# Spreading the output projections over single cycles, and moving the low-bit check of the weights, in an attention and feed-forward kernel

## The chip, the cores and the metric

The kernel runs on one core of a Trainium2 chip. The metric is the device time of one launch in microseconds (us), the median over several runs. Below, PE is TensorE (matrix products), DVE is VectorE, ACT is ScalarE, POOL is GpSimd and SP is SyncE, whose queue issues nearly all DMAs of this kernel.

## The reference, cut to what matters

```python
# x: (2, 1024, 512); 32 query heads, 8 key/value heads, head size 16
Q, K, V = x @ Wq.T + bq, x @ Wk.T + bk, x @ Wv.T + bv      # then split in heads
Q, K = _rope(Q, K);  K, V = repeat(K, 4), repeat(V, 4)
w = softmax(Q K^T / sqrt(16))
x = _layernorm(x + (w V) @ Wo.T + bo)                      # attention, post-norm
g = (x @ gate_w.T) * gate_s                                # gate_w, up_w: (1408, 512), ternary
u = (x @ up_w.T) * up_s
x = _layernorm(x + ((silu(g) * u) @ down_w.T) * down_s)    # down_w: (512, 1408), ternary
```

Everything is float32.

## The kernel before

**Attention.** The work is cut into 32 units: 2 batches, 2 halves of 512 queries, 8 key/value heads. A unit has 8 steps of 128 keys, so there are 256 steps, and the main loop takes two steps in each of its 128 cycles (`for c in range(STEPS // 2)`). For numerical reasons each score is made twice. The A pass (`max_pass`, L390) makes the scores with the queries in rows, and DVE reduces each to its maximum (`mx<-pa`, L398), 8 reductions a cycle; it runs 12 steps ahead (`LEAD`). The B pass (`exp_pass`, L432) makes the scores with the keys in rows, and ACT takes the exponential (L440). Then `av` (L453) multiplies by the values. After each unit `max_rows` (L405 to L414) brings the maxima into row form, by way of memory. In the last 6 cycles the A passes are all done (`alone`).

**Fills.** Into the head of each cycle (the letter F of the written order `WITH_FILL`) one piece of other matrix work is put, taken from the list `fill`. Up to cycle 28 these are the projections and transposes of Q, K and V. From cycle 36 on they belong to the rest of the layer, a quarter of 512 rows at a time. Quarter q starts at cycle 32(q + 1) + 4. It consists of the output projections (`project`, L560: four row tiles `t` of 128 rows), the transposition of the normalised rows (`x1_turn`, L592), 22 gate and up products (`hidden`, L611, in 11 blocks `f`, gate and then up), and four down products (`down`, L686, one for each row tile, 22 matmuls each). A quarter has 32 cycles, and this list has 30 entries, as each `project` handles two row tiles. So in two cycles of each of the first two quarters there is no fill, and the order is `NO_FILL`. Four quarters exist; the last one (`LASTQ`) has no attention left to lie beside, and is done after the loop, in a tail. The tail also takes the last two down products of quarter 2: the loop stops taking fills when two are left.

**The written order.** The order of instructions on every engine is that of the program (`tc.manual_schedule`); each engine executes its own in that order, and waits where an operand isn't ready. Small work (normalisation, gating, stores) is put off with `after(n, f)`, and is emitted at one of two points of each cycle, V0 and V1, by `v_hook`. V1 is about two thirds into the attention part of a cycle. SP's DMAs stand in one queue in that same order, so a DMA that waits for its data holds back those after it.

**Banks and buffers.** Seven PSUM banks go round among fills, A and B passes (`take` and `leave`); an eighth collects `av`. Weight tiles `wt` for the gate and up products are read from memory, one for each product, into a ring of `RING = 5` buffers; `hidden(i)` asks for tile i + RING - 1. The rows to which the attention's output is added are loaded by `load_residual` (DMA and an addition on POOL), of which the pool `fp5` holds five; the next quarter's are asked for by `more`, after the down products' rows are stored.

**Low bits.** The feed-forward weights are also rounded to a reduced format (float32r) in the first quarter of the loop: 33 pieces of 128x512 are loaded (`piece_load`, L174 and L179), rounded on ACT (`piece_round`, L184) and stored (L191). To see whether the rounding lost anything, DVE ORs the low 12 bits of each piece into a tile `low` (L186). `low_flag` reduces that tile to one number, in cycle 29. If it is not zero, the kernel does the whole feed-forward part again at full precision at the end (`feed_forward`); with the ternary weights of the reference it is zero.

Of the kernel before, what the change touches and what calls it, by code (L numbers as in the profile page):

```python
# [7 lines left out]
F32 = mybir.dt.float32  # L8
I32 = mybir.dt.int32
F32R = mybir.dt.float32r  # L10
AF = mybir.ActivationFunctionType
ALU = mybir.AluOpType
# [4 lines left out]
P = 128  # L17
B, T, D = 2, 1024, 512
# [6 lines left out]
NF = INTER // P  # L25
# [5 lines left out]
TH = HALF // P  # L31
# [6 lines left out]
US = NT  # L38
STEPS = len(UNITS) * US
QS = HKV * US  # L40
RING = 5
PIECES = 3 * NF
LOW = 0xFFF
LEAD = 12
# [2 lines left out]
def attn_ffn_kernel(tc, x, wqkv, bqkv, wo, bo, rope, wg, wu, wd, gs, us, ds, out):  # L47
    nc = tc.nc

    def pool(name, bufs=1, **kw):  # L50
        return tc.alloc_tile_pool(name=name, bufs=bufs, **kw)
# [7 lines left out]
    ap3 = pool("ap3", 3)  # L59
    wp = pool("wp", RING, side="right")  # L60
    qp1 = pool("qp1", side="right")
# [19 lines left out]
    def bank(name, shape=(P, HALF)):  # L81
        if psf[0] is None:
            return take("F", name, shape)
        p, tag = psf[0]
        return p.tile(list(shape), F32, tag=tag, name=name)
# [77 lines left out]
    low = ap1.tile([P, D], I32, name="low")  # L163
    flag = base.tile([1, 1], I32, name="flag")
    nc.gpsimd.memset(low, 0)
    SW, SR = {}, {}

    def piece_load(i):
        if i >= PIECES:
            return  # L170
        SW[i] = sp4.tile([P, D], F32, tag="sw", name="sw")
        if i < 2 * NF:
            f, up = divmod(i, 2)
            nc.sync.dma_start(  # L174
                out=SW[i].rearrange("p (c n) -> p c n", n=P),
                in_=(wu if up else wg)[:, :, f * P : (f + 1) * P],
            )
        else:
            nc.sync.dma_start(out=SW[i], in_=wd[:, i - 2 * NF, :])  # L179

    def piece_round(i):
        w = SW.pop(i)
        SR[i] = sp4.tile([P, D], F32R, tag="sr", name="sr")
        nc.scalar.copy(SR[i], w)  # L184

        nc.vector.scalar_tensor_tensor(  # L186
            low, w.bitcast(I32), LOW, low, ALU.bitwise_and, ALU.bitwise_or
        )

    def piece_store(i):  # L190
        nc.sync.dma_start(out=wsd[i], in_=SR.pop(i).bitcast(F32))  # L191
# [13 lines left out]
    def after(n, f):  # L205
        later.setdefault(now[0] + n, []).append(f)
# [237 lines left out]
    LASTQ = B * NH - 1  # L444
# [107 lines left out]
        mv, rs = sums(row)  # L552
        e.tensor_scalar(row, row, mv[:, 0:1], rs, ALU.subtract, ALU.mult)

    def project(q, t0):
        two = (t0, t0 + 1)
        py = {t: bank("py") for t in two}
        for c in range(NC):
            for t in two:
                nc.tensor.matmul(  # L560
                    py[t],
                    NUM[q, c][:, t * P : (t + 1) * P],
                    wo_sb[:, c, :],
                    start=c == 0,
                    stop=c == NC - 1,
                )
        for t in two:
            add_rows(q, t, py[t])
# [36 lines left out]
    def hidden(q, f, up):  # L605
# [3 lines left out]
        for c in range(NC):  # L609
            for k, x1 in enumerate(FP["x1"]):  # L610
# [6 lines left out]
                )  # L617
        ask_weights(i + RING - 1)
        if not up:
# [60 lines left out]
    def down(q, t, f0=0, f1=NF):  # L680
        if f0 == 0:
            FP["d", t] = bank("pd")
        pd = FP["d", t]
        for f in range(f0, f1):
            for k, h in enumerate(FP["h"]):
                nc.tensor.matmul(  # L686
                    pd,
                    h[:, f, t * P : (t + 1) * P],
                    wd_sb[:, f, :],
                    start=f == 0 and k == 0,  # L690
                    stop=f == NF - 1 and k == 1,
                )
        if f1 < NF:
            return
        end = q == LASTQ or now[0] >= 2 * STEPS
        ys = (FP["tmp"] if end else fp1).tile([P, D], F32, tag="ys", name="ys")
        if end:
            nc.vector.tensor_tensor(ys, pd, dsb, ALU.mult)
            nc.vector.tensor_tensor(XQ[q, t], ys, XQ[q, t], ALU.add)
            mv, rs = sums(XQ[q, t])  # L700
        else:
            nc.scalar.copy(ys, pd)
            nc.gpsimd.tensor_tensor(ys, ys, dsb, ALU.mult)
            nc.gpsimd.tensor_tensor(XQ[q, t], ys, XQ[q, t], ALU.add)
            after(2, lambda: norm(XQ[q, t], nc.gpsimd))

        def store():
            if end:
                row = XQ[q, t]
                nc.vector.tensor_scalar(row, row, mv[:, 0:1], rs, ALU.subtract, ALU.mult)  # L710
            b, qh = divmod(q, NH)
            r = qh * TH + t
            nc.sync.dma_start(out=out[b, r * P : (r + 1) * P, :], in_=XQ.pop((q, t)))
            after(2, more)

        def more():

            for i in range(TH):
                if q < LASTQ and (q + 1, i) not in DONE and i <= t + 1:
                    DONE.add((q + 1, i))  # L720
                    load_residual(q + 1, i)

        after(2 if end else 5, store)


    fill = [lambda m=m: qk_block(0, 1, m) for m in range(1, QK // P - 1)]
# [15 lines left out]
    fill = [(0, f) for f in fill]  # L742

    def quarter(q):
        first = (q + 1) * QS // 2 + 4
        fs = [lambda t=t: project(q, t) for t in (0, 2)]
        fs += [lambda t=t: (x1_turn(q, t), x1_turn(q, t + 1)) for t in (0, 2)]
        for f in range(NF):
            for up in (0, 1):
                fs.append(lambda a=(q, f, up): hidden(*a))  # L750
        downs = [(t, 0, NF) for t in range(TH)]
        if q == LASTQ:

            downs = [(0, 0, NF - 1), (1, 0, NF - 1), (0, NF - 1, NF), (1, NF - 1, NF), (2, 0, NF)]
        for a in downs:
            fs.append(lambda a=a: down(q, *a))
        if q == LASTQ:
            fs.append(lambda: last_down(q, TH - 1))
        return [(first, f) for f in fs]
# [89 lines left out]
    for c in range(STEPS // 2):  # L849
        probs = {}  # L850

        pieces = range(*(min(max(0, (i - 2) * PIECES // (QS // 2 - 5)), PIECES) for i in (c, c + 1)))
        for i in pieces:
            piece_round(i)
        if pieces:
            after(1, lambda ps=pieces: [(piece_store(i), piece_load(i + 4)) for i in ps])
        alone = 2 * c + LEAD >= STEPS
        has_fill = bool(fill) and fill[0][0] <= c
        if c >= (STEPS - QS) // 2:
            has_fill = has_fill and len(fill) > 2  # L860
        for s in NO_A if alone else WITH_FILL if has_fill else NO_FILL:
            if s == "F":
                if has_fill:
                    fill.pop(0)[1]()
                    leave("F")
                continue
            n = 2 * c + int(s[-1])
            if s[0] == "V":
                v_hook(n)
                if before is not None:  # L870
                    av(n - 2, before[n - 2])
                continue
            j, i = int(s[1]), "abc".index(s[2])
            if s[0] == "A":
                max_pass(n + LEAD, j, i)
                continue
            if i == 2 and n not in probs:
                probs[n] = ap3.tile([P, G, HALF], F32, tag="prob", name="prob")
            exp_pass(n, j, i, probs.get(n))
        before = probs  # L880
        u, s = divmod(2 * c + 1, US)
        if s == US - 1 and u + 3 < len(UNITS):
            prep(u + 3)
        if (2 * c + 1 + LEAD) % US == US - 1 and not alone:
            max_rows((2 * c + 1 + LEAD) // US)
        if 0 <= (f := c - QS // 2 - 4) < NF:
            nc.sync.dma_start(out=wd_sb[:, f, :].bitcast(F32), in_=wsd[2 * NF + f])
        if c == QS // 4:
            load_weights()
        if c == QS // 2 - 3:  # L890
            low_flag()
        if c == QS // 2 - 2:
            sp4.release()
            qp4.release()
            qp2.release()
            qp1.release()
            fp1 = pool("fp1", side="right")
            fp4 = pool("fp4", 4, side="right")
            fp5 = pool("fp5", 5, side="right")
            wd_sb = fp1.tile([P, NF, D], F32R, name="wd_sb")  # L900
            FP["tmp"] = fp1
            for i in range(RING):
                after(i + 11, lambda i=i: ask_weights(i))
            for t in range(TH):
                after(t + 1, lambda t=t: load_residual(0, t))
            for q in range(B * NH - 1):
                fill.extend(quarter(q))
# [11 lines left out]
    ps_x = pool("ps_x", 8, space=PSUM)  # L919
    psf[0] = (ps_x, "px")  # L920

    del fill[-2:]
    rest = [(0, lambda a=a: down(LASTQ - 1, *a)) for a in ((2, 0, NF), (3, 0, 8), (3, 8, NF))]
    last = quarter(LASTQ)
    while later:
        v_hook(min(later))
    fill += [rest[0], *last[0:2], rest[1], *last[2:4], rest[2]]
    n = 2 * STEPS

    def drain():  # L930
# [135 lines left out]
```

## Time and profile before

| | |
|---|---|
| Median of 3 runs | 1137.92 us (1136.79 to 1137.92) |
| The profiled execution: its own time | 1135.88 us |
| its span, first to last instruction | 1134.0 us |
| mean granted clock of TensorE | 0.997 |
| busy: PE, DVE, ACT, POOL | 1109.4, 819.3, 703.4, 384.1 us |
| first quarter of the loop and cycles 29 to 35 | to 322.92 us |
| quarter 0, quarter 1 (from the first projection to the next quarter's) | 252.21, 252.20 us |
| DVE's low-bit operations (33, from 82.4 to 272.8 us) | 23.7 us |

The times of the stages are read from the chain of waits in order of time, in which each fill of a cycle has a row with its start. A fill's row starts a cycle, so the distance of two such rows is the length of a cycle. The busy time of PE is modelled at the ends of instructions, so the lengths of cycles tell more than the busy share.

### The profile page before, as it was taken

The page shows a single profiled execution, that of the slowest core. Times are in us where ns is not written, and L with a number is a line of the kernel's source. Part 1 is how long each engine was busy: PE and PEld are TensorE (multiplying, and loading weights), DVE is VectorE, ACT ScalarE, POOL GpSimd, SP SyncE. Part 2 cuts the span into 40 slices and gives each one's busy share as a digit, 9 for nine tenths or more (in the row PEclk, how much of TensorE's full clock was granted, in tenths as well). Part 3 has the DMA queues.
Part 4 walks back from the last instruction along what each step waited for, and adds up shares of the span by engine and source line. Part 5 has one row for each costly group of instructions (what it writes and reads, how often), then busy time and mean ns, then how long its engine had stood idle before and what let it go on. Part 6 is the DMA issues. An engine that isn't in the chain of part 4 may idle for free.

```text
span 1134.0 us, 23242 instructions
## 1 busy us (share of the span) xinstructions
PE 1109.4 (98%) x8894; PEld 590.9 (52%) x8894; DVE 819.3 (72%) x1481; ACT 703.4 (62%) x1312; POOL 384.1 (34%) x411
## 2 busy tenths in 40 slices
PE   7999999999999999999999999999999999999997
PEld 5534545555444555555544555555544555545686
DVE  4968888988867777776658777776668778722634
ACT  3148777776746777775547777775537777783251
POOL 4473441442124222223524222224535222235332
PEclk9999999999999999999999999999999999999999
DMA  6577666664424332220222222220323222111331
GB/s 180 165 240 229 198 216 204 211 212 147 87 68 146 123 115 85 83 84 30 81 86 97 86 86 86 83 87 24 98 66 106 87 87 87 50 53 66 105 118 40
DMA packets 98919, 127.60 MB, mean 113 GB/s; under 512 B 26873, under 2 KB 51194, under 8 KB 98674
## 3 DMA queue, kind: packets, MB, share of 16 engines
q1 hardware_dynamic: 98450, 125.72, 36.1%
q8 instruction: 72, 1.18, 0.4%
q10 hardware_dynamic: 352, 0.33, 0.1%
q14 instruction: 45, 0.37, 0.1%
HBM read 83.56 MB, written 36.93 MB: 106 GB/s over the span
## 4 chain that ended last, share of the span: by engine, by line
PE 89%; DVE 8%; issue 1%; POOL 0%; ACT 0%; DMA 0%; ACTq 0%; POOLq 0%; SPq 0%; DVEq 0%
PE pv L453 21%; PE pa L390 21%; PE pg L611 15%; PE pb L432 13%; PE pd L686 7%; DVE mx L398 5%; PE py L560 5%; PE pq L259 5%; DVE st L539 1%; PE pv L318 1%; PE pt L244 1%; PE px L592 0%; PE pd L661 0%; DVE xq L582 0%; DVE rot L280 0%
## 5 line engine op out<-in xcount | busy, mean ns | idle before, releaser
L398 DVE TENSOR_REDUCE mx<-pa 128x1 f32<-128x512 f32 x1024 | 646.3, 684 | 174.9 <-PE pa L390 104.1
L440 ACT ACTIVATE prob<-pb 128x512 f32<-128x512 f32 x1024 | 540.7, 600 | 198.8 <-PE pb L432 157.4
L390 PE MATMUL pa<-KS,QH 32*128 32x512 f32 x1024 | 334.7, 449 | 4.1 <-DVE mx L398 2.9
L432 PE MATMUL pb<-QH,KS 32*128 32x512 f32 x1024 | 304.1, 460 | 4.9 <-DVE mx L398 4.2
L390 PE MATMUL pa<-KS,QL 32*128 32x512 f32 x1024 | 306.9, 407 | 0.0
L453 PE MATMUL pv<-prob,va 128*32 128x512 f32 x2048 | 272.9, 604 | 0.0
L432 PE MATMUL pb<-QL,KS 32*128 32x512 f32 x1024 | 271.3, 417 | 0.0
L432 PE MATMUL pb<-mt,ones 32*128 32x512 f32 x1024 | 243.4, 394 | 0.0
L390 PEld LDWEIGHTS pa<-KS,QH 32*128 32x128 f32 x1024 | 145.7, 182 | 156.5 <-DVE mx L398 109.1
L642 POOL TENSOR_TENSOR z<-pus,z 128x512 f32<-128x512 f32 x44 | 56.4, 1283 | 389.4 <-ACT pus L639 362.3
L432 PEld LDWEIGHTS pb<-QL,KS 32*128 32x128 f32 x1024 | 127.3, 183 | 93.4 <-issue 92.2
L390 PEld LDWEIGHTS pa<-KS,QL 32*128 32x128 f32 x1024 | 158.6, 183 | 19.0 <-issue 9.2
L432 PEld LDWEIGHTS pb<-QH,KS 32*128 32x128 f32 x1024 | 129.6, 182 | 31.4 <-DVE mx L398 18.6
L611 PE MATMUL pg<-x1h,wt 128*128 128x512 f32 x352 | 144.6, 411 | 0.0
L432 PEld LDWEIGHTS pb<-mt,ones 32*128 32x128 f32 x1024 | 138.8, 183 | 2.0
L611 PE MATMUL pg<-x1l,wt 128*128 128x512 f32 x352 | 137.9, 392 | 0.3 <-DVE x1l L596 0.3
L453 PEld LDWEIGHTS pv<-prob,va 128*32 128x32 f32 x2048 | 40.8, 108 | 93.5 <-issue 82.0
L611 PEld LDWEIGHTS pg<-x1h,wt 128*128 128x128 f32 x352 | 66.0, 187 | 37.1 <-issue 11.6
L259 PE MATMUL pq<-xT,wqkv_sb 128*128 128x256 f32 (+1 forms) x248 | 79.5, 462 | 3.4 <-DVE xT L247 1.2
L611 PEld LDWEIGHTS pg<-x1l,wt 128*128 128x128 f32 x352 | 66.2, 188 | 12.8 <-DVE x1l L596 0.8
L277 POOL TENSOR_TENSOR t<-q,cosT 128x256 f32<-128x256 f32 (+1 forms) x31 | 31.0, 999 | 108.9 <-ACT q L275 106.3
L686 PE MATMUL pd<-wd_sb,hh 128*128 128x512 f32 x165 | 66.0, 400 | 0.7 <-ACT o L469 0.7
(100 smaller groups left out, 1013.5 us busy)
## 6 DMA issues: line engine op xcount, KB each, us to landing
wt<-wsd SPq DMA_DIRECT2D x88, 256.0 KB
KS<-kT SPq DMA_DIRECT2D x124, 128.0 KB
wsd<-sr SPq DMA_DIRECT2D x33, 256.0 KB
QH<-qT SPq DMA_DIRECT2D x31, 256.0 KB
QL<-qT SPq DMA_DIRECT2D x31, 256.0 KB
qT<-hi SPq DMA_DIRECT2D x18, 256.0 KB
qT<-lo SPq DMA_DIRECT2D x18, 256.0 KB
xs<-in_x_dram SPq DMA_DIRECT2D x16, 256.0 KB
```

The lines of the kernel that those rows point to most:

```text
L244: nc.tensor.transpose(pt[:, c, :], xs[:, c * P : (c + 1) * P], ident)
L259: nc.tensor.matmul(pq, wqkv_sb[:, c, m * P : (m + 1) * P], XT[b, half][:, c, t0 * P : t1 * P], start=c == 0, stop=c == NC - 1,)
L277: nc.gpsimd.tensor_tensor(t1_, q, cosT[:, ns], ALU.mult)
L390: nc.tensor.matmul(PA[n, j], (QH, QL)[i][u][r, t * P : (t + 1) * P], KS[u][r, half * HALF : (half + 1) * HALF], start=i == 0, stop=i == 1,)
L398: nc.vector.tensor_reduce(MX[u][:, t, j, half : half + 1], PA.pop((n, j)), AX.X, ALU.max)
L432: nc.tensor.matmul(PB[n, j], ones[r, :] if i == 2 else KS[u][r, kc * P : (kc + 1) * P], (QH[u], QL[u], mts[u % 2])[i][r, :], start=i == 0, ...
L440: nc.scalar.activation(prob[:, j, :], PB.pop((n, j)), AF.Exp, scale=SCALE)
L453: nc.tensor.matmul(PV[u][j * E : (j + 1) * E, :], vas[b][:, kc, g, :, :].rearrange("p d o -> p (d o)"), prob[:, j, :], start=done == 0, st ...
L560: nc.tensor.matmul(py[t], NUM[q, c][:, t * P : (t + 1) * P], wo_sb[:, c, :], start=c == 0, stop=c == NC - 1,)
L611: nc.tensor.matmul(p, w[:, c, :], x1[:, c, :], start=c == 0 and k == 0, stop=c == NC - 1 and k == 1,)
L642: nc.gpsimd.tensor_tensor(z, pus, z, ALU.mult)
L686: nc.tensor.matmul(pd, h[:, f, t * P : (t + 1) * P], wd_sb[:, f, :], start=f == 0 and k == 0, stop=f == NF - 1 and k == 1,)
```

## The change

There are two parts.

One concerns the fills. `project` takes one row tile at a time in quarters 0, 1 and 2, so that each of these has four entries for the projections, in four cycles, where it had two. Their lists have 32 entries then, and no cycle is without fill between quarters. The loop now stops taking fills when four are left, so that all four down products of quarter 2 go to the tail. There the order is two downs, the projections, one down, the transposes, one down; before it was one down, the projections, the first 8 of 11 blocks of the other, the transposes, the last 3 blocks. In the tail `project` still takes two row tiles.

The other concerns the low bits. The operation on DVE leaves `piece_round`; ACT's rounding stays. A new function `check_bits` reads each piece once more from memory, into one buffer `raw`, and does the operation when it is called the next time. It is called in three of four cycles from cycle 39 on, and acts at V1 of the cycle that follows; the 33 operations lie in cycles 41 to 84. First it does the operation on the piece that is there, then it issues the read of the next into the same buffer. `low_flag` moves to cycle 96. `RING` is 4 instead of 5.

```diff
-RING = 5
+RING = 4
...
+    def piece_read(i, to):
         if i < 2 * NF:
             f, up = divmod(i, 2)
             nc.sync.dma_start(
-                out=SW[i].rearrange("p (c n) -> p c n", n=P),
+                out=to.rearrange("p (c n) -> p c n", n=P),
                 in_=(wu if up else wg)[:, :, f * P : (f + 1) * P],
             )
         else:
-            nc.sync.dma_start(out=SW[i], in_=wd[:, i - 2 * NF, :])
+            nc.sync.dma_start(out=to, in_=wd[:, i - 2 * NF, :])
...
         nc.scalar.copy(SR[i], w)
 
-        nc.vector.scalar_tensor_tensor(
-            low, w.bitcast(I32), LOW, low, ALU.bitwise_and, ALU.bitwise_or
-        )
+    RAW = [None, 0]
+
+    def check_bits():
+        if RAW[0] is not None:
+            nc.vector.scalar_tensor_tensor(
+                low, RAW[0].bitcast(I32), LOW, low, ALU.bitwise_and, ALU.bitwise_or
+            )
+            RAW[0] = None
+        if RAW[1] < PIECES:
+            RAW[0] = fp1.tile([P, D], F32, tag="raw", name="raw")
+            piece_read(RAW[1], RAW[0])
+            RAW[1] += 1
...
-    def project(q, t0):
-        two = (t0, t0 + 1)
+    def project(q, *two):
...
-        fs = [lambda t=t: project(q, t) for t in (0, 2)]
+        if q == LASTQ:
+            fs = [lambda t=t: project(q, t, t + 1) for t in (0, 2)]
+        else:
+            fs = [lambda t=t: project(q, t) for t in range(TH)]
...
-            has_fill = has_fill and len(fill) > 2
+            has_fill = has_fill and len(fill) > TH
...
-        if c == QS // 2 - 3:
+        if QS // 2 + 6 <= c < 3 * QS // 2 and c % 4 != 2:
+            after(2, check_bits)
+        if c == 3 * QS // 2:
+            assert RAW == [None, PIECES]
             low_flag()
...
-    del fill[-2:]
-    rest = [(0, lambda a=a: down(LASTQ - 1, *a)) for a in ((2, 0, NF), (3, 0, 8), (3, 8, NF))]
+    rest = fill[-TH:]
+    del fill[-TH:]
     last = quarter(LASTQ)
...
-    fill += [rest[0], *last[0:2], rest[1], *last[2:4], rest[2]]
+    fill += [*rest[0:2], *last[0:2], rest[2], *last[2:4], rest[3]]
```

## The prediction

> **What bounds the kernel now.** I read the page first, then the chain of waits in order of time, the table of stretches, and the timelines of VectorE and SyncE where the chain left TensorE. On the page, the busy row and the slices:
>
> ```profile
> PE 1109.4 (98%) x8894; PEld 590.9 (52%) x8894; DVE 819.3 (72%) x1481; ACT 703.4 (62%) x1312; POOL 384.1 (34%) x411
> PE   7999999999999999999999999999999999999997
> DVE  4968888988867777776658777776668778722634
> ```
>
> TensorE (PE) is busy nearly always, so moving its work gains nothing unless it closes a stall. A mean cannot show those, the chain can. A loop cycle is what lies between two fills at its head. The chain around the end of a quarter (start, us, what):
>
> ```profile
> 540.83 5.21 PE pd L686 x22
> ...
> 551.18 5.21 PE pd L686 x22
> ...
> 575.13 7.08 PE py L560 x16
> ...
> 587.99 7.08 PE py L560 x16
> ...
> 600.85 1.03 PE px L592 x8
> ```
>
> A cycle with a down product takes 551.18 - 540.83 = 10.35 us: 5.21 of fill and 5.14 of attention. Cycles with a gate or up product take 7.18 in the same view (2.04 + 5.14). So 5.14 is what attention costs when TensorE sets the pace. A cycle with two projections takes 587.99 - 575.13 = 12.86 = 7.08 + 5.14 + 0.64, so 0.64 is a stall. A down cycle from 551.18 ends at 561.53; the two cycles without fill then last to 575.13, 13.60 in all, or 6.80 each against 5.14: 1.66 lost in each. A turn cycle takes 6.73 (600.85 to 607.58, the next fill of the chain), 0.57 over 1.02 + 5.14. The table of stretches (PE, PEld, DVE, ACT, POOL busy) says who holds the unfilled cycles:
>
> ```profile
> 561.53:575.13 13.60, 12.76 (x113) 6.03 (x112) 12.76 (x25) 8.49 (x18) 4.87 (x5) 1.00 0.30 91
> 540.83:551.18 10.35, 10.35 (x79) 6.27 (x79) 5.72 (x11) 5.33 (x11) 5.47 (x5) 1.00 0.43 128
> ```
>
> VectorE is busy 12.76 of 13.60 us in them, but 5.72 of 10.35 in a down cycle. Both limits exist; fill placed in an unfilled cycle is nearly free up to 1.66 us, and costs its full TensorE time beyond.
>
> **One projection a cycle.** A projection of one row tile is half of 7.08, 3.54 us, so its cycle is 5.14 + 3.54 = 8.68 if nothing stalls. Is the 0.64 gone? In the old cycle VectorE does two additions, two statistics and two aggregates; the second pair is in front of the third reduction:
>
> ```profile
> 584.10 0.68 DVE L539 BATCH_NORM_STATS2 st<-xq 128x6 f32<-128x512 f32 x1
> 584.82 0.18 DVE L544 BATCH_NORM_AGGREGATE mv<-st 128x2 f32<-128x6 f32 x1
> 584.92 0.66 DVE L539 BATCH_NORM_STATS2 st<-xq 128x6 f32<-128x512 f32 x1
> 585.62 0.18 DVE L544 BATCH_NORM_AGGREGATE mv<-st 128x2 f32<-128x6 f32 x1
> 585.72 1.85 DVE L398 TENSOR_REDUCE mx<-pa 128x1 f32<-128x512 f32 x3
> ```
>
> With one tile the reductions at 585.72 come 0.8 us earlier, more than the 0.64 that was lost. I take 8.68; bounds are no stall and the old 0.64 (not below nothing, since TensorE is then full).
> Quarters 0 and 1 each swap two double projections and two unfilled cycles for four single ones: 4 x 8.68 - 2 x 12.86 - 13.60 = -4.6 us, twice. The four additions of the next residual on POOL and their loads stay where they were relative to the down products, but the first projection now follows at once. In the last down cycle (start S) the load is issued near S+6.2 behind an output store on SP; with some 2.5 us to land and the row 1.26 for the addition (behind POOL's two 1.3 us down steps) the row is ready near S+10; VectorE wants it at S + 10.35 + 3.6. That slack of 4 us hides it.
> Quarter 2 has no unfilled cycle. Its 28 remaining fills become 4 projections, 2 turns and 22 products, instead of 2, 2, 22 and 2 downs. The last six cycles have no score pass for the maximum: there a down cycle takes 1028.21 - 1019.21 = 9.00 and a product cycle (1019.21 - 995.73) / 4 = 5.87. Change: 4 x 8.68 + 2 x 5.87 - 2 x 12.86 - 2 x 9.00 - 2 x 7.18 = -11.6 us. Most of that is work postponed.
>
> **Four downs at the end.** The chain of the tail, and SyncE's timeline there:
>
> ```profile
> 1040.23 5.32 PE pd L686 x22
> 1045.55 13.73 PE py L560 x32
> 1059.28 3.67 PE pd L686 x16
> ...
> 1064.10 2.50 DVE x1l L596 x4
> ...
> 1066.64 40.00 PE pg L611 x175
> ```
>
> ```profile
> 1070.41 0.34 SPq L713 DMA_DIRECT2D out_dram<-xq  x1
> 1070.80 1.88 SPq L532 DMA_DIRECT2D wt<-wsd  x4
> ```
>
> TensorE already has no hole for two more downs: the projections start right behind the down at 1040.23, with no wait for the reciprocals. So two downs cost 2 x 5.2 = +10.4. One gain: the last down, now whole behind the turns, covers x1l, for which the first product waited 0.5 us (66.64 instead of 66.14): -0.5. One loss: RING is 4. SP's order in the changed program has the store of the last down in front of all 19 weight loads of the quarter. That store waits for the normalised row, 3.9 us after VectorE starts on the down (1066.50 to 1070.41). With four buffers only three weight tiles are there when the products begin, so the fourth is issued 4.6 us in and needed after 3 x 1.82 = 5.46 us (40.00/22 = 1.82 a product). Before, the fifth was issued 4.4 us in and needed after 7.3, without a stall, so it lands in under 2.9 us. The packets of that load were through 1.6 us after the issue, of a later one 2.2: stall 0.7 to 1.3, I take 1.0. The Trainium skill (DMA: Bandwidth & Descriptors, section Anatomy of one DMA) gives 2.0 us fixed plus bytes over 436 GB/s, 2.6 us for 256 KB, for DMAs that GpSimd issues; this would make it 1.7. I keep the trace's. Later loads have 5.46 us from issue to need. In the loop three tiles ahead are 21 us. Tail: +10.4 - 0.5 + 1.0 = +10.9.
>
> **Low bits out of the first quarter.** 33 operations of VectorE (23.7 us) leave it; the rounding on ScalarE stays. Filled cycles there take 7.07 (1.93 + 5.14), so TensorE hides most of the 23.7. Excess in the chain: 102.48 to 117.97 and 132.11 to 147.61 are two cycles of 15.5, 1.35 over each; in each VectorE did the maxima's row work and then
>
> ```profile
> 112.08 1.79 DVE L186 SCALAR_TENSOR_TENSOR low<-sw,low 128x512 int32<-128x512 int32 x2
> ```
>
> Four cycles with one such operation behind the row work are 0.21 over (199.04 to 206.32 for one). Four turn cycles are 0.2 to 0.3 over the 6.73 of later ones, 1.1 in all, of which I count half. Sum 2.7 + 0.85 + 0.55 = -4.1 (bounds 0, if ScalarE's copies hold those cycles, and -4.7).
>
> **Low bits in later quarters.** The same 33 operations come at the second V point of three cycles in four, each followed by a 256 KB read on SP's queue, from cycle 41 to 84; no view shows them there. The nearest row is a gate cycle now:
>
> ```profile
> 380.85 1.89 DVE L398 TENSOR_REDUCE mx<-pa 128x1 f32<-128x512 f32 x3 [0.38 <-PE pa L390]
> 382.66 0.24 DVE L486 RECIPROCAL rc<-rc 128x16 f32<-128x16 f32 x1
> 382.82 0.63 DVE L631 SCALAR_TENSOR_TENSOR z<-th,z 128x512 f32<-128x512 f32 x1
> 383.43 1.89 DVE L398 TENSOR_REDUCE mx<-pa 128x1 f32<-128x512 f32 x3
> 386.36 1.29 DVE L398 TENSOR_REDUCE mx<-pa 128x1 f32<-128x512 f32 x2 [1.04 <-PE pa L390]
> ```
>
> An operation of 0.63 us at that very point costs this cycle nothing, and 1.04 us of idle time follow the next three reductions. The low-bit operation takes 0.68 (median of its tile's view), and fits. Bounds: 0 (it adds work, so no gain), and 1.35 for each of the 17 gate cycles that then hold two such operations, the worst pair of the first quarter, 23 us. I take 0, the nearer row.
> The rule against it: the Trainium skill (SBUF — State Buffer, section SBUF: two separate sides) says that a VectorE operation with two SBUF inputs and a GpSimd operation lock each other out for a whole instruction. Here the longest of the 33 took 1.19 against 0.68, beside POOL's 1.15 us product: the trace agrees. By the rule each could wait up to POOL's 1.28, 42 us in all. By the trace POOL works on a product from 372.11 to 375.41 in an up cycle that begins at 369.27, and the V point comes at about 375.6; in gate cycles POOL rests. The three in projection cycles meet its 2.1 us normalisation, with 3.54 us of TensorE fill behind them; the three in turn cycles meet POOL busy (10.43 of 13.45 us from 348.65), at most 3 x 1.28 = 4 us. I add nothing, and keep the 4 for the range.
> Each read goes out when its operation has released the one buffer, and is due 7.18 us later. SP waits for that operation in its order, with the next weight load (21 us ahead), the maxima's rows and the attention operands behind it, all due cycles later. The operands' 1 MB burst falls in the cycle that is left out. DMA is 0.33 busy there: nothing.
>
> **Sum.** -4.6 - 4.6 - 11.6 + 10.9 - 4.1 = -14.0 us. The working is of the profiled execution (span 1134.0, 1135.88 with what lies around it), which would become 1121.9; the median of the runs shown is 2.0 above it, 1137.92, so I predict 1123.9.
>
> **Rivals.** (a) Slower: the second V point has no room for two operations, and gate cycles stall as the two in the first quarter did: 17 x 1.35 = 23 against 14, 1146.9. It decides from 14.0 / 33 = 0.42 us of stall for each operation, by lag or by a read that lands over 6.5 us after its issue. For it: those two cycles. Against: the 1.04 us of idle time, and that z is there today for nothing. Chance 0.06. (b) Single projection cycles stall as the double ones: 12 x 0.64 = 7.7, 1131.6. Against: the 0.8 us above. 0.12. (c) The first quarter does not get shorter: 1128.0. For: cycles with one low-bit operation and no row work run at 7.07 already. 0.15. (d) Late weights in the tail or small stalls at the new reads, 0.1 us each: about 1127. 0.10. (e) All cancel: some 14 us of stalls of several kinds, no change. 0.02. My forecast 0.55, within about 2 us of 1123.9.
>
> **How the numbers follow.** About 0.2% (2.3 us) can be told from no change. Faster: all but (a) and (e), 0.92; same 0.02; slower 0.06. The range runs from 1120.5 (all 4.7 of the first quarter, no late weight, and the 1.1 us by which the runs differ make 1121.2; some turn cycles may shorten too) to 1131.5, up to the edge of (b), and leaves out (a), (e) and half of (b).
>
> **What would show it.** Right: the first projections of quarters 0, 1 and 2 about 247.6 us apart instead of 252.2; product cycles still 7.18 from cycle 42 to 85; the unfilled pairs at 561 and 814 gone; the two 15.5 us pairs of the first quarter at 14.1; the tail from the last probabilities to the end 11 us longer, with one idle spot of a microsecond before the fourth product that ends with a DMA of wt. Wrong: product cycles over 7.4 with TensorE waiting for mx, VectorE idle before the low-bit operation for its read, projection cycles over 9.2, or a repeated wait for wt.

## The result, and the profile after

The changed kernel is slower: 1146.25 us (median of 5 runs, 1143.24 to 1148.57) against 1137.92, ratio 1.0076 with a 95% interval of 1.0061 to 1.0091. The forecast was 1123.9. The profiled execution took 1145.74 us, its span is 1143.8.

The busy row of the page after, and TensorE's slices:

```profile
PE 1112.1 (97%) x8894; PEld 589.7 (52%) x8894; DVE 823.0 (72%) x1487; ACT 702.6 (61%) x1310; POOL 373.6 (33%) x405
PE   7999999999998999999998999999999999999997
```

The sums tell almost nothing; only two of TensorE's slices fall to 8, those from 343 and from 600 us. The stages do, from the table of stretches (each from its first projection to the next quarter's):

| stage | before | after | change | foreseen |
|---|---|---|---|---|
| up to the first projection | 322.9 | 318.8 | -4.1 | -4.1 |
| quarter 0 | 252.2 | 255.7 | +3.5 | -4.6 |
| quarter 1 | 252.2 | 257.1 | +4.9 | -4.6 |
| quarter 2, to the end of the loop | 209.7 | 204.0 | -5.7 | -11.6 |
| tail | 97.0 | 108.2 | +11.3 | +10.9 |

The first stage and the tail came as foreseen, and the three quarters did not. Laying out the cycles by the heads of their fills shows that nearly all the difference lies in one cycle of each: the fourth projection cycle takes 15.4, 17.2 and 14.1 us (cycles 39, 71 and 103), where the other three take 8.78. That is 20.3 us. The rest is as it was forecast: product cycles are 7.18 (but for five of 7.52), the unfilled cycles between quarters are gone, the pairs of 15.5 in the first quarter are 14.15.

The chain of waits in order of time, in the worst of the three cycles, leaves TensorE for a long way (start, us, what):

```profile
600.46 1.58 ACT prob L454 x3
602.05 0.48 SPq L490
...
602.58 2.17 DMA sd<-o
...
604.76 0.32 SPq L512
...
605.17 2.80 DMA raw<-in_wd_dram
...
608.00 0.04 DVE low L195
608.04 0.57 issue
608.61 0.70 DVE mx L412
```

What SyncE's queue did then (timeline of SP in the changed kernel):

```profile
583.40 0.59 SPq L177 DMA_DIRECT2D raw<-in_wu_dram  x1
602.01 0.52 SPq L490 DMA_DIRECT2D num<-o  x1
602.58 0.55 SPq L497 DMA_DIRECT2D sd<-o  x1
603.22 0.39 SPq L726 DMA_DIRECT2D out_dram<-xq  x1
603.70 0.46 SPq L535 DMA_DIRECT2D xq<-in_x_dram  x1
604.76 0.32 SPq L512 DMA_DIRECT2D rc<-sd  x1
605.17 0.38 SPq L182 DMA_DIRECT2D raw<-in_wd_dram  x1
```

and VectorE (timeline, with the idle time before an instruction and what ended it in brackets):

```profile
598.46 1.85 DVE L412 TENSOR_REDUCE mx<-pa 128x1 f32<-128x512 f32 x3
607.12 0.25 DVE L500 RECIPROCAL rc<-rc 128x16 f32<-128x16 f32 x1 [6.80 <-DMA rc<-sd]
608.00 0.69 DVE L195 SCALAR_TENSOR_TENSOR low<-raw,low 128x512 int32<-128x512 int32 x1 [0.63 <-DMA raw<-in_wd_dram]
608.61 1.88 DVE L412 TENSOR_REDUCE mx<-pa 128x1 f32<-128x512 f32 x3
```

SP issues nothing for 18 us, between 583.99 and 602.01. What it waits with is `num<-o`: the numerators of the first unit of the next quarter. `num` has four buffers, one for each chunk of the output projection, so this store goes into the buffer of chunk 0 of the quarter that is just being projected. The store is written at the second V point of the first projection cycle. Before, two cycles with two projections each had read that buffer for the last time soon after the head of the second; now the fourth cycle reads it, two cycles later. The fourth cycle's first matmuls begin at 600.8, and SP goes on 1.2 us later, when chunk 0 is read. All DMAs behind the store have waited, among them `rc<-sd`, for which VectorE stands in front of its reciprocal. Behind the reciprocal stand the low-bit operation and the reductions of the score banks; with no free bank TensorE stops, until 609.35. The timeline of TensorE shows the cycle's fill, the pause, and the fill of the next cycle, 17.15 us after the first:

```profile
600.82 3.70 PE L573 MATMUL py<-wo_sb,num 128*128 128x512 f32 x8
...
609.35 0.49 PE L446 MATMUL pb<-QH,KS 32*128 32x512 f32 x1 [4.40 <-DVE mx L412]
...
617.97 1.09 PE L605 MATMUL px<-ident,xq 128*128 128x128 f32 x8
```

In the kernel before, the same store is issued at 589.93, 1.9 us after the second projection cycle began, and `rc` follows at once:

```profile
589.93 0.53 SPq L476 DMA_DIRECT2D num<-o  x1
590.51 0.52 SPq L483 DMA_DIRECT2D sd<-o  x1
592.67 0.32 SPq L498 DMA_DIRECT2D rc<-sd  x1
```

TensorE's pause has an echo. The table of stretches, before the stall and behind the pause (PE, PEld, DVE, ACT, POOL busy, then the granted clock):

```profile
593.00:600.40 7.40, 7.40 (x61) 3.19 (x61) 6.15 (x14) 2.93 (x6) 0.00 (x0) 1.00 0.00 0
...
611.34:614.40 3.06, 3.06 (x21) 1.21 (x22) 2.14 (x5) 1.09 (x3) 2.87 (x4) 0.50 0.48 115
```

From 2 us after the pause the granted clock is 0.50 for 3 us; a group of eight value matmuls that takes 1.00 us elsewhere in the chain takes 1.86 there.

### The profile page after: what moved, and what is told of

It reads as the page before. It is cut to its first block, busy times and chain, and to the rows that moved or that the text cites. A ratio compares the mean times of both kernels' runs of the same rounds, so it can differ in the third digit from the quotient of the medians.

```text
span 1143.8 us, 23282 instructions
## 1 busy us (share of the span) xinstructions
PE 1112.1 (97%) x8894; PEld 589.7 (52%) x8894; DVE 823.0 (72%) x1487; ACT 702.6 (61%) x1310; POOL 373.6 (33%) x405
## 4 chain that ended last, share of the span: by engine, by line
PE 88%; DVE 4%; DMA 4%; SPq 1%; POOL 1%; ACT 1%; issue 1%; POOLq 0%; DVEq 0%; ACTq 0%
PE pv L467 22%; PE pa L404 21%; PE pb L446 14%; PE pg L624 13%; PE pd L699 7%; PE pq L273 5%; PE py L573 4%; DVE mx L412 2%; DMA wt<-wsd 1%; PE px L605 1%; PE pv L332 1%; DMA sd<-o 1%; SPq L361 1%; PE pd L674 0%; PE pt L258 0%
## 5 line engine op out<-in xcount | busy, mean ns | idle before, releaser
L446 PE MATMUL pb<-QH,KS 32*128 32x512 f32 x1024 | 303.0, 463 | 11.9 <-DVE mx L412 11.3
L467 PE MATMUL pv<-prob,va 128*32 128x512 f32 x2048 | 276.2, 611 | 0.0
L624 PEld LDWEIGHTS pg<-x1h,wt 128*128 128x128 f32 x352 | 66.0, 187 | 40.4 <-issue 10.9
L699 PE MATMUL pd<-wd_sb,hl 128*128 128x512 f32 x165 | 64.3, 390 | 0.0
```

Source lines behind the costliest of these rows:

```text
L446: nc.tensor.matmul(PB[n, j], ones[r, :] if i == 2 else KS[u][r, kc * P : (kc + 1) * P], (QH[u], QL[u], mts[u % 2])[i][r, :], start=i == 0, ...
L467: nc.tensor.matmul(PV[u][j * E : (j + 1) * E, :], vas[b][:, kc, g, :, :].rearrange("p d o -> p (d o)"), prob[:, j, :], start=done == 0, st ...
L624: nc.tensor.matmul(p, w[:, c, :], x1[:, c, :], start=c == 0 and k == 0, stop=c == NC - 1 and k == 1,)
L699: nc.tensor.matmul(pd, h[:, f, t * P : (t + 1) * P], wd_sb[:, f, :], start=f == 0 and k == 0, stop=f == NF - 1 and k == 1,)
```

## The experiments

The theory: the numerators' buffer is held until the fourth projection cycle, SP's queue stands behind its store, and VectorE waits for DMAs out of that queue. The rivals: the low-bit operations or their second reads hold VectorE in the projection cycles; residual rows arrive late; spreading the projections costs in itself. Each ratio below is to the kernel before, run beside it (medians 1137.40 to 1138.51 us).

**Five buffers for the numerators**

```diff
-    ap4 = pool("ap4", 4)
+    ap4 = pool("ap4", 5)
```

> The changed kernel with five num buffers instead of four (12 KB more of SBUF), nothing else. Theory (the first unit of the next quarter stores its numerators into the buffer that the fourth projection still has to read, so SP's queue stands until the fourth projection cycle and VectorE with it): the fourth projection cycles of quarters 0, 1, 2 fall from 15.4, 17.2, 14.1 to 8.8 us, 20.3 us in all, and the time to about 1126. Rival (the low-bit operations or their reads in the projection cycles stall): no change, 1146. Rival (residual rows are late for the projections): no change, 1146.

(One such buffer is 128x512 in float32: 2 KB of each of the 128 partitions, and not the 12 KB of the expectation.)

Measured: 1125.15 us, ratio to before 0.9887 (0.9870 to 0.9903). All twelve projection cycles take 8.77 to 8.79 us. The fourth of quarter 1, which took 17.15, in the chain:

```profile
592.52 3.63 PE py L573 x8
...
601.29 0.81 PE px L605 x6
```

SP in the same place:

```profile
575.41 0.59 SPq L177 DMA_DIRECT2D raw<-in_wu_dram  x1
576.10 0.57 SPq L490 DMA_DIRECT2D num<-o  x1
576.72 0.55 SPq L497 DMA_DIRECT2D sd<-o  x1
577.37 0.39 SPq L726 DMA_DIRECT2D out_dram<-xq  x1
577.84 0.38 SPq L535 DMA_DIRECT2D xq<-in_x_dram  x1
579.91 0.32 SPq L512 DMA_DIRECT2D rc<-sd  x1
```

The store follows the read in 0.7 us, the queue runs on, and 21 us are gone. Nothing else was touched: the second reads, the operations and the residual rows are all where they were. The first two rivals fall as the cause of the loss, and single projection cycles at 8.78 leave nothing for the third.

**The store put off instead**

```diff
-        nc.sync.dma_start(out=num[rows, :], in_=o[0:P:2, :])
+        hold = 5 if g == 0 and 0 < q else 0
+        if hold:
+            after(hold, lambda: nc.sync.dma_start(out=num[rows, :], in_=o[0:P:2, :]))
+        else:
+            nc.sync.dma_start(out=num[rows, :], in_=o[0:P:2, :])
```

> The changed kernel with four num buffers, but the store of the numerators of a quarter's first unit is put off by five V points, to the cycle of the fourth projection, so that the later DMAs go ahead of it in SP's queue. Theory (it is the queue that stands, not the store itself that is missed): as with five buffers, about 1126, fourth projection cycles at 8.8 us. If the store itself were needed early: 1146 or later. Rivals (low-bit reads, late residual rows): 1146.

Measured: 1125.28 us, 0.9888 (0.9870 to 0.9906). Four buffers, and the store is as late as in the changed kernel; but the others are ahead of it:

```profile
577.42 0.56 SPq L501 DMA_DIRECT2D sd<-o  x1
578.07 0.39 SPq L730 DMA_DIRECT2D out_dram<-xq  x1
578.55 0.38 SPq L539 DMA_DIRECT2D xq<-in_x_dram  x1
580.06 0.32 SPq L516 DMA_DIRECT2D rc<-sd  x1
...
595.31 0.54 SPq L492 DMA_DIRECT2D num<-o  x1
```

So the late store itself hurts nobody. It was its place in the queue.

**The projections alone**

The low-bit operation back in `piece_round`, no second reads, `low_flag` in cycle 29, `RING = 5`; `project` by single tiles and four downs in the tail as in the changed kernel.

> Only the part with the projections and the four downs in the tail: low bits in the first quarter as before, no second read, RING 5. Theory: the fourth projection cycles stay at 14 to 17 us; the first quarter is 4.9 us longer than in the changed kernel, five cycles of 7.52 and the late weight in the tail are gone (-1.7, -2): about 1147. Rival (low-bit operations or reads): the three cycles at 8.8, about 1126.

Measured: 1147.91 us, 1.0081 (1.0058 to 1.0104). The fourth cycles take 16.2, 15.8 and 14.8 us. The stall belongs to this part, with no second read in the kernel.

**The hold alone**

The kernel before, with empty fills between its two double projections, two in quarter 0 and one in quarter 1; as many of the unfilled cycles at the end of the quarter go.

```diff
+        fs[1:1] = [lambda: None] * (2 - q if q < 2 else 0)
```

> The kernel before with one edit: the second double projection of quarter 0 waits two cycles (two cycles without fill in between, the two that it has at the end of the quarter otherwise), that of quarter 1 one cycle. No single projections, no low bits moved, no additional work. Theory: in quarter 0 the buffer is held to cycle 39, as in the changed kernel, and the cycle of the second projections is 5 to 8 us longer; in quarter 1 it is held one cycle, SP is released some 10 us before VectorE's reciprocal is due, and nothing is lost: about 1144. Rivals (single projections, low bits): as before, 1138.

Measured: 1141.42 us, 1.0032 (1.0019 to 1.0044). Right in kind, too high in size. SP stands from 327.4 to 351.67 in quarter 0 and VectorE waits 8.62 us, about as long as in cycle 39 of the changed kernel (8.03). First this run, then the changed kernel:

```profile
357.32 0.25 DVE L486 RECIPROCAL rc<-rc 128x16 f32<-128x16 f32 x1 [8.62 <-DMA rc<-sd]
```

```profile
352.65 0.25 DVE L500 RECIPROCAL rc<-rc 128x16 f32<-128x16 f32 x1 [8.03 <-DMA rc<-sd]
```

but the cycle is 15.79 us instead of 12.86, a loss of 2.9, where cycle 39 lost 6.6. TensorE's pauses are 1.39 and 0.35 us here, with the granted clock at 1.00 behind them; in cycle 39 the pause is 4.26 us, and the clock is 0.57 in the 2 us behind it. A double projection keeps TensorE busy for 7.08 us at the head of the cycle without needing VectorE, a single one for 3.54; that would explain the shorter pause. It follows from the two timelines and was not tried by itself. In quarter 1 the second projections take 13.39, 0.5 more than before: a hold of one cycle costs next to nothing.

**The low bits alone**

The kernel before with `check_bits` as in the changed kernel, and `RING = 4`.

> Only the part with the low bits: the kernel before with the low-bit operations and second reads in cycles 41 to 84 and RING 4; double projections, two unfilled cycles and the short tail stay. Theory (this part holds no buffer of the numerators): first quarter -4.9 us, five cycles of three operations at one V point +1.7, a late weight tile in the tail +1.5, a little in the unfilled cycles: about 1136.5. Rival (the low bits share in the loss of 8 us): over 1138.

Measured: 1137.61 us, 0.9989 (0.9978 to 1.0001), not to be told from no change. The five cycles of 7.52 us and the late weight are there; the first quarter is shorter as foreseen. What I had called a little in the unfilled and turn cycles is not so little: cycle 66, without fill, takes 8.60 instead of 7.59, and turn cycles 70 and 71 take 7.02 and 7.43 instead of 6.73. In cycle 70 one low-bit operation (at 604.85) takes 1.42 us instead of 0.68; it began inside a product of POOL (604.44 to 605.72). In the changed kernel the unfilled cycles no longer exist, and its turn cycles stay at 6.72. So this part alone earns nothing measurable, and no part of the 8 us is its own.

**Three projection cycles**

```diff
-            fs = [lambda t=t: project(q, t) for t in range(TH)]
+            fs = [lambda a=a: project(q, *a) for a in ((0,), (1,), (2, 3))]
```

> The changed kernel with the projections in three cycles: one tile, one tile, two tiles. The buffer is then read for the last time in the third cycle, not in the fourth. Theory: SP is released near the head of the third cycle, some 10 us before VectorE's reciprocal is due in it, and no cycle over 13.5 us is left; with a double cycle again and one unfilled cycle in each quarter about 1130. Rival (any spread of the projections costs): over 1140.

Measured: 1128.62 us, 0.9915 (0.9887 to 0.9943). The projection cycles take 8.78, 8.78 and 12.86 us in all three quarters, and the rival that any spread costs falls. In quarter 1 SP issues the store at 586.67 and `rc<-sd` at 589.47, and the reciprocal starts at 597.07 without a wait. The last read one cycle earlier is enough.

**The reciprocal later**

```diff
-            after(k + 2, inverse)
-            after(2 * k + 2, spread)
+            d = 2 if g == 0 else 0
+            after(k + 2 + d, inverse)
+            after(2 * k + 2 + d, spread)
```

> The changed kernel with four num buffers; only the reciprocal of a quarter's first unit (and of every even unit), and what follows from it, comes two V points later on VectorE. SP's queue stands as long as before. Theory (the wait reaches TensorE by the reciprocal, behind which VectorE's reductions stand): most of the 20 us goes, at most a few us are left for the maxima's rows and the low-bit read that come out of the queue late: 1127 to 1132. If TensorE waited for something else out of the standing queue (maxima, attention operands): 1140 to 1146.

(The edit moves the reciprocal of a quarter's first unit only, `g == 0`; the other even units stay.)

Measured: 1138.69 us, 0.9999 (0.9987 to 1.0012): 7.6 us under the changed kernel, where I had expected 14 to 19. The fourth cycles take 8.78, 16.3 and 11.7 us. In quarter 0 the reciprocal was all there was. In quarter 1 the next in VectorE's order stands in its place, and in quarter 2 the one after that:

```profile
603.70 0.69 DVE L195 SCALAR_TENSOR_TENSOR low<-raw,low 128x512 int32<-128x512 int32 x1 [7.82 <-DMA raw<-in_wd_dram]
...
859.39 0.69 DVE L596 TENSOR_TENSOR xq<-py,xq 128x512 f32<-128x512 f32 x1 [5.07 <-POOL xq L537]
```

The second is the addition of the fourth tile's residual row, loaded by a DMA that was also behind the store.

**The reciprocal later, and no second read in the hold**

The same, with `and c not in (68, 69)` in the condition of `check_bits`.

> The kernel with the late reciprocal, and besides no low-bit reads asked for in the second and third projection cycles of quarter 1 (they follow later; all 33 are done). Theory (what VectorE waits for is whatever stands behind the numerators' store in SP's queue: the reciprocal first, the low-bit read second, the residual row of the fourth tile third): the fourth projection cycle of quarter 1 falls from 16.3 to about 11.7 us, what the residual row costs in quarter 2, where there is no low-bit read; that of quarter 0 stays at 8.8; the time is some 4.6 us under that of the late reciprocal alone, near 1134. If the read was not the carrier: 16 us in that cycle and no gain.

Measured: 1134.4 us, 0.9972 (0.9961 to 0.9983), 4.3 us less than without the second edit (3.1 by the two ratios, since the kernel before was 1.1 us faster beside this one). The fourth cycle of quarter 1 falls to 13.15 us, and the wait that is left is the one that quarter 2 has:

```profile
604.15 0.69 DVE L596 TENSOR_TENSOR xq<-py,xq 128x512 f32<-128x512 f32 x1 [5.13 <-POOL xq L537]
```

It does not fall to the expected 11.7, though TensorE pauses only 1.60 us; the granted clock behind the pause is 0.69 from 605 to 608 and 0.81 to 612. In this execution, the slowest of the eight (1138.24 us), the fourth cycle of quarter 2 takes 13.79 us too, where it took 11.7 before; the last section returns to this.

Three instructions in VectorE's order need something from behind the store. Taking one away uncovers the next; releasing the queue frees all.

**A version that beats both**

The store put off as above; one line ahead of the tail's first `drain()`, so that the fourth weight tile of the last quarter is asked for before the tail's stores; and one more condition, so that no low-bit operation falls on the V point of the numerators' division.

```diff
-        if QS // 2 + 6 <= c < 3 * QS // 2 and c % 4 != 2:
+        if QS // 2 + 6 <= c < 3 * QS // 2 and c % 4 != 2 and c % 8 != 3:
...
+    ask_weights(LASTQ * 2 * NF + RING - 1)
     drain()
```

> The late store of the numerators, and two small things: the fourth weight tile of the last quarter is asked for before the tail's stores go into SP's queue, and the low-bit operation leaves out the cycles in which the division of the numerators falls on the same V point. Theory: 1125.3, less 2.0 for the late tile and 1.7 for five cycles of 7.52: about 1121.6.

Measured: 1121.9 us, 0.9862 (0.9830 to 0.9894). No product cycle is over 7.25 us, and the products of the tail run in one piece in the chain:

```profile
1050.62 40.03 PE pg L628 x176
```

## Why the prediction was wrong

It failed at one step, in the part "One projection a cycle". It says there "I take 8.68; bounds are no stall and the old 0.64", and of the DMAs it follows only the residual rows ("That slack of 4 us hides it"). Its own sign of being wrong, projection cycles over 9.2 us, came in one cycle of each quarter. It asked what a projection needs, and not what it holds; and the slack was that of the first tile's row, where the fourth tile's load stood behind the store. What a moved step frees later was taken as nothing without a reason: the `num` buffer's release moved two cycles, and the next writer of that buffer is a DMA in the in-order queue that everything else uses. None of the rivals named it, and the upper bound of 0.64 for each cycle (rival b, 7.7 us) was no bound. The runs put 20.3 us in that place: 1146.25 with four buffers, 1125.15 with five.

That 21.1 us is the whole error but for 1.3: with the queue free the kernel takes 1125.15, and 1123.9 was forecast. The other terms:

- Single projection cycles: 8.78 in every experiment with a free queue, 8.68 was taken. The 0.64 of the double ones is gone, as forecast; that the second pair of statistics was its cause was argued, and not tried by itself.
- The swap with unfilled cycles and the turns: in the version that beats both, quarters 0 and 1 take 248.04 and 248.11 us against 252.2, and 247.6 was forecast.
- First quarter: right in sum, not in all its parts. It got 4.9 us shorter, and the loop began 0.8 later (57.65 instead of 56.86). The two cycles of 8.4 and the four of 7.28 fell to 7.07. The turn cycles there did not move (6.94 to 7.05 before and after), so the half of 1.1 that I counted was nothing; two unfilled cycles, 30 and 34, lost 0.6 each, which I had not counted.
- Low bits at the second V point: two operations there cost nothing, as argued from the gate cycle. I had not seen that in five of these cycles the division of the numerators is a third. VectorE's timeline in one:

```profile
394.62 0.68 DVE L516 TENSOR_TENSOR num<-num,den 128x512 f32<-128x512 f32 x1
395.22 0.69 DVE L195 SCALAR_TENSOR_TENSOR low<-raw,low 128x512 int32<-128x512 int32 x1
395.82 0.69 DVE L644 SCALAR_TENSOR_TENSOR z<-th,z 128x512 f32<-128x512 f32 x1
396.42 3.20 DVE L412 TENSOR_REDUCE mx<-pa 128x1 f32<-128x512 f32 x5
```

The cycle that begins behind it takes 7.52 instead of 7.18; five times 0.34 is 1.7 us. The lock that the prediction weighed did not show in the changed kernel, where the longest of the 33 took 0.693 us, but it did in other versions. With the low bits alone one operation took 1.42 us, and in the second version with the late reciprocal one took 1.41, begun at 616.24 inside a product of POOL (615.82 to 617.10). Each was in a turn cycle, and the cycle that began behind it took 7.43 and 7.26 us instead of 6.73. That is inside the 4 us that were kept for the range; that it did not come in the changed kernel is luck. The wait for the second read was real only where the queue stood.

- Tail: +11.3 against +10.9. The late weight cost 0.8 more than taken, the rest 0.4 less. The chain there:

```profile
1078.47 0.34 SPq L726
...
1078.86 2.80 DMA wt<-wsd
...
1081.79 34.74 PE pg L624 x152
```

TensorE waits 1.8 us at 1081.79 (the view of waits). From the packets I took 1.0; the load landed 2.80 us after its issue, and the estimate by the Trainium skill (DMA: Bandwidth & Descriptors, Anatomy of one DMA), 1.7, which I set aside as being for another issuer, was the nearer one. The end of the packets was not yet the landing that the engine saw: in two stretches of 0.4 us from 1079.2 the DMA engines moved 271 and 369 GB/s, together the 256 KB of one load, and TensorE went on at 1081.79. (That these bytes are all of the first load is an assumption.)

## What to carry to other kernels

When a step is spread or moved later, list what it holds as well as what it needs: every buffer whose last reader it is, the next writer of that buffer, and what stands behind that writer in its queue. A DMA that waits for a buffer in an in-order queue makes every later DMA late, and with it whichever instruction of each engine comes first that needs one; removing that instruction only uncovers the next. An additional buffer, or the waiting DMA put behind its neighbours, cost no time here and freed them all.

## What the runs showed of the hardware

A pause of TensorE cost more than itself here. After the pause that ended at 609.35 the granted clock was 0.61 until 611.3, 0.50 until 614.4 and 0.69 until 618, where it is 1.00 nearly everywhere else; the mean clock of the whole execution fell from 0.997 to 0.990, and it is 0.999 in the version that beats both. Of the 8.4 us that the worst cycle lost, 4.4 are the pause, and 4.0 came when TensorE was at work again: from 609.35 what was left of the attention part took until 617.97, 8.6 us, where the whole of it takes 5.14. Length times clock of the three stretches (1.95, 3.06 and 3.57 us) makes 5.2 us at full clock, so by this estimate the lower clock took 3.4 of the 4.0 us; VectorE's backlog may have the rest.

The Trainium skill (TensorE: Matmul & The Clock Gate, Part 1: The HAM clock gate) describes this as a gate that halves the clock after an idle window of about 3.4 us. The half clock agrees, the length does not: in quarter 2 of the changed kernel the clock was 0.50 from 865.9 to 868.5 after a pause of 2.63 us. The two kernels with the late reciprocal are the same in the fourth projection cycle of quarter 2, and TensorE pauses 1.54 us there in one and 1.56 in the other. In one the clock stayed at 1.00, and the cycle took 11.65 us; in the other it was 0.50 from 860 to 864, and the cycle took 13.79. So here a pause of 1.6 us could halve the clock, and did not always; what decided it the runs do not show.
